# Layer 1's softmax sums: a pair's first eight blocks summed by VectorE in place of TensorE

## The chip, the cores and the metric

The kernel runs on one core of a Trainium2 chip. The metric is the time of one execution on the device in microseconds (us). Before the change it was 3967.98 us (median of 3 runs, 3965.11 to 3968.51).

## The reference

Two graph layers run on 4096 nodes of 512 features; only the second matters here. It is a masked attention with 8 heads of 64:

```python
q = jnp.einsum('nd,hdk->hnk', node_matrix, Wqs)      # k, v alike
scores = jnp.einsum('hqk,hmk->hqm', q, k) * kd ** (-0.5)
scores = scores + IDENTITY_BIAS * eye - MASK_VAL * (1.0 - adj)
att = jax.nn.softmax(scores, axis=-1)
return jnp.einsum('hqm,hmk,hko->qo', att, v, Wo)
# then x = layernorm(x + that)
```

The softmax needs, for every query and head, the sum of the weights over all 4096 keys. The change is about who forms that sum.

## The kernel before

Queries are taken in 8 groups of 512, heads in 4 pairs. Such a "pair" `(g, m)` meets its keys in 32 blocks `j` of 128. For a block TensorE makes scores (keys on the partitions, queries along the free axis), ScalarE takes the exponential in place, VectorE multiplies by the mask into a weight tile `p` of 128 x 1024, and TensorE multiplies `p` by the values. A sum over keys is one over the 128 partitions and the 32 blocks. GpSimd adds 24 of the blocks elementwise into `q_sum`; TensorE sums the other eight straight from `p`, with a column of ones:

```python
def by_tensor(j):
    return j % 6 in (2, 3) and j < BY_PE              # BY_PE = 24: blocks 2 3 8 9 14 15 20 21

def weigh(g, m, j, s):
    nc.scalar.activation(s, s, AF.Exp)
    p = wp.tile([P, HP, G], F32, name="p1", bufs=10)
    # ... cut: the mask
    nc.vector.tensor_tensor(p, s, mask.to_broadcast([P, HP, G]), op=ALU.mult)
    pt[g, m, j] = p
    if by_tensor(j) or j == 0:
        return
    # ... cut: j == 1 starts q_sum
    nc.gpsimd.tensor_tensor(q_sum[g, m], q_sum[g, m], p, op=ALU.add)

def close1(g, t, s):                                  # finishes one output tile
    # ... cut: y = x + s on VectorE; mean and variance; 1/sd and nb on GpSimd
    nc.gpsimd.tensor_scalar(nb, nb, -1.0, None, op0=ALU.mult)

    def normalise():
        nc.scalar.activation(y, y, AF.Identity, bias=nb, scale=rs)
        nc.sync.dma_start(out[i * P:(i + 1) * P, :], y)
    later.at(2, normalise)
```

A step takes three blocks (the eleventh, the tail, takes two) and issues them in this order:

```python
got = [scores(*u) for u in batch]                     # three score buffers in all
# ... cut, in the tail: sums of the pair before, projection of one output tile
for u, su in zip(batch, got):
    weigh(*u, su)
if extra_sum:  divide(*extra_sum, den_ps)             # GpSimd: on = o_sb * r
if extra_tile: close1(*extra_tile, y_ps[:, 0, :])
for g, m, j in last:                                  # the batch of the step before
    products(g, m, j)
# ... cut: column sums, copy of the finished output
later.step()                                          # at(2): at the end of the next step
```

So the normalisation of a tile that closes in a tail stands, in ScalarE's program, behind the exponentials of the next pair's blocks 0 to 2 and ahead of those of blocks 3 to 5.

Of the kernel before, what the change touches and what calls it, by code (L numbers as in the profile page):

```python
# [8 lines left out]
F32 = mybir.dt.float32  # L9
BF16 = mybir.dt.bfloat16  # L10
I32 = mybir.dt.int32
AF = mybir.ActivationFunctionType
ALU = mybir.AluOpType
AX = mybir.AxisListType
# [3 lines left out]
P = 128  # L18
# [411 lines left out]
def tile_gat_then_masked_attention(  # L430
# [16 lines left out]
    nc = tc.nc  # L447
    N, D = x.shape
    H0, D0, _ = weight_u.shape
    H1, _, KD = wks.shape  # L450
    NT = N // P
    G = 512
# [2 lines left out]
    KC = D // P  # L455
    HP = P // KD
    NP1 = H1 // HP
    QD = P // 4
    CH = 8
    NCH = NT // CH  # L460
    W0 = D0 + 1
# [9 lines left out]
    const = main.enter_context(tc.tile_pool(name="const", bufs=1))  # L471
# [9 lines left out]
    ones = const.tile([P, KD], F32, name="ones")  # L481
# [2 lines left out]
    nc.vector.tensor_scalar(ident_e, ident, 1.0100501670841679, None, op0=ALU.mult)  # L484
    least = const.tile([P, NG * NP1], F32, name="least")
    total = const.tile([P, NG * NP1], F32, name="total")
    pick = const.tile([P, HP, KD], F32, name="pick")
    nc.gpsimd.memset(pick, 0.0)
    for e in range(HP):
        for n in range(2):  # L490
            r = (n * HP + e) * QD
            nc.gpsimd.memset(pick[r:r + 1, e, :], 1.0)

    base_d = [dram.tile([P, D], F32, name=f"base_d{i}") for i in range(NT)]
    x1_d = [dram.tile([P, D], F32, name=f"x1_d{i}") for i in range(NT)]
# [31 lines left out]
    with tc.tile_pool(name="l0", bufs=1) as l0, \  # L527
# [41 lines left out]
        with tc.tile_pool(name="l0s", bufs=2) as sp, \  # L569
# [56 lines left out]
            for g in range(NG):  # L626
# [4 lines left out]
                for c in range(KC):  # L631
                    p = ps.tile([P, GT, P], F32, name="t_ps")
# [9 lines left out]
                for t in range(GT):  # L642
# [3 lines left out]
                    for c in range(KC):  # L646
                        nc.tensor.matmul(s_ps, xT[:, c, t * P:(t + 1) * P], w_sb[:, c, :],
                                         start=(c == 0), stop=(c == KC - 1))
                    b_ps = ps.tile([P, D], F32, name="b_ps")
                    for c in range(KC):  # L650
                        nc.tensor.matmul(b_ps, xT[:, c, t * P:(t + 1) * P], pw_sb[:, c, :],
                                         start=(c == 0), stop=(c == KC - 1))
# [6 lines left out]
                    for k, f in ((0, f1[:, i, :]), (1, f2[:, i, :])):  # L659
# [3 lines left out]
                                                op=ALU.mult)  # L663
# [19 lines left out]
        with tc.tile_pool(name="l0w", bufs=2) as wp, \  # L683
# [3 lines left out]
            fr_t, sup_t, agg_t, az_t, o_t, p_t = {}, {}, {}, {}, {}, {}  # L687
# [95 lines left out]
            for n, (w, h, j) in enumerate(steps):  # L783
# [6 lines left out]
                u = h * NT + j  # L790
# [3 lines left out]
                p = p_t.pop((w, h, j))  # L794
                for t in range(WT):
                    nc.tensor.matmul(o[t // BK][:, t % BK, :], p[:, t * P:(t + 1) * P],  # L796
                                     sup_t[w, h][:, j, :],
                                     start=(j == 0 and t % BK == 0), stop=(j == NT - 1),
# [9 lines left out]
    with tc.tile_pool(name="l1", bufs=1) as l1:  # L808
        wo_sb = l1.tile([P, KC, D], F32, name="wo_sb")

        with tc.tile_pool(name="l1s", bufs=2) as sp, \
# [17 lines left out]
            for g in range(NG):  # L829
# [4 lines left out]
                for m in range(NP1):  # L834
                    k_ps = ps.tile([P, G], F32, name="k_ps")
                    for c in range(KC):
                        nc.tensor.matmul(k_ps, w3["wk"][:, c, m * P:(m + 1) * P], xT[:, c, :],  # L837
                                         start=(c == 0), stop=(c == KC - 1))
# [4 lines left out]
                    for c in range(KC):  # L843
                        nc.tensor.matmul(q_ps, w3["wq"][:, c, m * P:(m + 1) * P], xT[:, c, :],  # L844
                                         start=(c == 0), stop=(c == KC - 1))
# [4 lines left out]
                for t in range(GT):  # L850
                    v_ps = ps.tile([P, D], F32, name="v_ps")
                    for c in range(KC):
                        nc.tensor.matmul(v_ps, xT[:, c, t * P:(t + 1) * P], w3["wv"][:, c, :],
                                         start=(c == 0), stop=(c == KC - 1))
# [8 lines left out]
        with tc.tile_pool(name="l1w", bufs=2) as wp, \  # L863
                tc.tile_pool(name="l1p", bufs=1, space=PSUM) as ps:
            NB = 3
            BY_PE = 24
            kt, vt, qt, at, mdt, pt, q_sum, o_t, o_sb, sm_t, sm_sb, on_t = (
                {} for _ in range(12))
            later = Later()

# [4 lines left out]
            def of_group(g, j0, j1):  # L875
                r = g * G % W
                return adjT_d[g * G // W][:, j0:j1, r:r + G]

            def load_adjT(g, c):
                at[g, c] = wp.tile([P, CH, G], BF16, name="adjT1", bufs=NCH + 2)  # L880
                nc.sync.dma_start(at[g, c], of_group(g, c * CH, (c + 1) * CH))

            def load_md(g):
# [53 lines left out]
                                     start=True, stop=True)  # L937
                return s

            def by_tensor(j):  # L940

                return j % 6 in (2, 3) and j < BY_PE

            def weigh(g, m, j, s):
                nc.scalar.activation(s, s, AF.Exp)  # L945
                p = wp.tile([P, HP, G], F32, name="p1", bufs=10)
                if j // GT == g:
                    mask = mdt[g][:, j % GT, None, :]
                else:
                    mask = at[g, j // CH][:, j % CH, None, :]  # L950
                nc.vector.tensor_tensor(p, s, mask.to_broadcast([P, HP, G]), op=ALU.mult)  # L951
                pt[g, m, j] = p
                if by_tensor(j) or j == 0:
                    return
                if j == 1:
                    q_sum[g, m] = wp.tile([P, HP, G], F32, name="q_sum")
                    nc.gpsimd.tensor_tensor(q_sum[g, m], pt[g, m, 0], p, op=ALU.add)
                else:
                    nc.gpsimd.tensor_tensor(q_sum[g, m], q_sum[g, m], p, op=ALU.add)  # L959

            def products(g, m, j):
                if j == 0:
                    o_t[g, m] = ps.tile([P, G], F32, name="o1_ps")
                o = o_t[g, m]
                p = pt[g, m, j]
                v = vt[g, m, j // CH]
                for e in range(HP):
                    r = slice(e * KD, (e + 1) * KD)
                    nc.tensor.matmul(o[r, :], v[:, j % CH, r], p[:, e, :],  # L969
                                     start=(j == 0), stop=(j == NT - 1))  # L970

            def sums(g, m, j):


                if j == 3:
                    sm_t[g, m] = ps.tile([P, G], F32, name="sm_ps")
                for n in range(2):
                    for e in range(HP):
                        r = (n * HP + e) * QD
                        nc.tensor.matmul(sm_t[g, m][r:r + QD, :], ones[:, 0:QD],  # L980
                                         pt[g, m, j - 1 + n][:, e, :],
                                         start=(j == 3), stop=(j + 6 >= BY_PE))

            def all_sums(g, m, s):
                q = q_sum.pop((g, m))
                sm = sm_sb.pop((g, m))
                for e in range(HP):
                    nc.tensor.matmul(s[e * KD:(e + 1) * KD, :], ones, q[:, e, :],
                                     start=True, stop=False)
                for e in range(HP):  # L990
                    nc.tensor.matmul(s[e * KD:(e + 1) * KD, :], pick[:, e, :], sm,
                                     start=False, stop=True)

            def divide(g, m, s):
                if m == 0:
                    on_t[g] = wp.tile([P, NP1, G], F32, name="on")
                den = wp.tile([P, G], F32, name="den1")
                nc.scalar.activation(den, s, AF.Copy)
                r = wp.tile([P, G], F32, name="r1")
                n = index[g, m, 0] // NT  # L1000

                nc.vector.tensor_reduce(least[:, n:n + 1], den, AX.X, ALU.min)  # L1002
                nc.vector.tensor_reduce(total[:, n:n + 1], den, AX.X, ALU.add)  # L1003
                nc.vector.reciprocal(r, den)  # L1004
                nc.gpsimd.tensor_tensor(on_t[g][:, m, :], o_sb.pop((g, m)), r, op=ALU.mult)  # L1005
# [5 lines left out]

            def close1(g, t, s):
                i = g * GT + t
                y = wp.tile([P, D], F32, name="y1", bufs=4)
                nc.sync.dma_start(y, x1_d[i])
                nc.vector.tensor_tensor(y, y, s, op=ALU.add)  # L1016

                mv, rs = moments(y)
                nb = small.tile([P, 1], F32, name="nb")
                nc.gpsimd.tensor_tensor(nb, mv[:, 0:1], rs, op=ALU.mult)  # L1020
# [6 lines that stand above are left out]
# [7 lines left out]
            def step(batch, extra_sum, extra_tile):  # L1034
                got = [scores(*u) for u in batch]
                if extra_sum:
                    den_ps = ps.tile([P, G], F32, name="sm_ps")
                    all_sums(*extra_sum, den_ps)
                if extra_tile:
                    y_ps = ps.tile([P, HP, G], F32, name="s_ps", bufs=NB)  # L1040
                    project(*extra_tile, y_ps[:, 0, :])
                for u, su in zip(batch, got):
                    weigh(*u, su)
                if extra_sum:
                    divide(*extra_sum, den_ps)
                if extra_tile:
                    close1(*extra_tile, y_ps[:, 0, :])
                for g, m, j in last:
                    products(g, m, j)
                for g, m, j in last:  # L1050
                    if by_tensor(j) and j % 6 == 3:
                        sums(g, m, j)
                        if j + 6 >= BY_PE:
                            sm_sb[g, m] = wp.tile([P, G], F32, name="sm_sb")
                            nc.scalar.activation(sm_sb[g, m], sm_t.pop((g, m)), AF.Copy)
                    if j == NT - 1:
                        o_sb[g, m] = wp.tile([P, G], F32, name="o_sb")
                        nc.scalar.activation(o_sb[g, m], o_t.pop((g, m)), AF.Copy)
                last[:] = batch
                later.step()  # L1060
# [66 lines left out]
```

## Time and profile before

| | before |
|---|---|
| median of the runs | 3968.12 us |
| TensorE busy (PE) | 3799.8 us, 96% |
| VectorE (DVE) / ScalarE (ACT) / GpSimd (POOL) busy | 2532.6 / 1855.8 / 2046.3 us |
| one pair of layer 1, with a tile to close | 68.29 us |

Busy shares are averages over two layers with different limits. The useful unit is one pair, read from the timeline of each engine; the lines are in the prediction. In such a line the first number is the start in us from the start of the span, the second the time to the end of a merged run, and what stands in brackets is the idle time ahead of the run and what ended it.

### The profile page before, as it was taken

The numbers are of one execution on the slowest core, as the hardware profiler recorded it, in microseconds if no ns is written. First come the engines' busy times: TensorE is split into PE (matmuls) and PEld (weight loads), VectorE is DVE, ScalarE is ACT, GpSimd is POOL, SyncE is SP. The second block draws the span as 40 slices with busy tenths as digits, with TensorE's granted clock in tenths as the row PEclk, the third lists the DMA queues.
The fourth block names the chain that finished last, engine by engine and source line by source line (L and its number), as shares of the span: only waits on it lengthen the run. The fifth ranks groups of instructions, "written<-read, shape, count | busy, mean of one in ns | idle before, by whom it ended". The sixth has DMA issues, their size and how long they took to land. (4 is left out here: it accounts for less than half of the span.)

```text
span 3967.4 us, 51832 instructions
## 1 busy us (share of the span) xinstructions
PE 3799.8 (96%) x20490; PEld 1985.2 (50%) x20490; DVE 2532.6 (64%) x2432; ACT 1855.8 (47%) x2113; POOL 2046.3 (52%) x1211
## 2 busy tenths in 40 slices
PE   7988998999989889989999999999999999999998
PEld 3448998989989734433333333333333333333332
DVE  3447998988989801125666666666666666666665
ACT  1226767767656510024444444444444444444443
POOL 2320012021030100018888888888887888888886
PEclk9998999999999989999999999999999999999999
DMA  6885566656431143242222322322323223223211
GB/s 163 193 199 162 131 195 157 175 161 160 150 109 63 43 148 111 98 146 83 96 83 80 117 83 79 113 88 78 109 74 114 80 88 117 80 77 115 75 63 54
DMA packets 232429, 447.47 MB, mean 113 GB/s; under 512 B 21744, under 2 KB 136688, under 8 KB 225008
## 3 DMA queue, kind: packets, MB, share of 16 engines
q1 hardware_dynamic: 179264, 386.38, 29.4%
q0 software_dynamic: 42432, 51.39, 7.8%
q10 hardware_dynamic: 10480, 6.29, 0.5%
q8 instruction: 163, 2.67, 0.3%
q14 instruction: 90, 0.74, 0.1%
HBM read 372.51 MB, written 100.86 MB: 119 GB/s over the span
## 5 line engine op out<-in xcount | busy, mean ns | idle before, releaser
L959 POOL TENSOR_TENSOR q_sum<-q_sum,p 128x1024 f32<-128x1024 f32 x704 | 1659.0, 2356 | 332.6 <-DVE p L951 287.2
L951 DVE TENSOR_TENSOR p<-s_ps,adjT 128x1024 f32<-128x1024 f32 x896 | 1043.8, 1217 | 686.1 <-ACT s_ps L945 669.1
L945 ACT ACTIVATE s_ps<-s_ps 128x1024 f32<-128x1024 f32 x1024 | 971.1, 1009 | 1004.2 <-PE s_ps L936 1004.1
L796 PE MATMUL o_ps<-sup_t,p 128*128 128x129 f32 x8192 | 966.0, 279 | 42.4 <-DVE p L719 42.4
L936 PE MATMUL s_ps<-q_sb,k_sb 64*128 64x512 f32 x4096 | 981.6, 610 | 16.8 <-issue 10.2
L796 PEld LDWEIGHTS o_ps<-sup_t,p 128*128 128x128 f32 x8192 | 941.5, 194 | 52.2 <-issue 29.6
L969 PE MATMUL o_ps<-p,v_sb 128*64 128x512 f32 x4096 | 956.5, 601 | 0.0
L936 PEld LDWEIGHTS s_ps<-q_sb,k_sb 64*128 64x128 f32 x4096 | 367.6, 187 | 628.4 <-issue 388.4
L719 DVE SCALAR_TENSOR_TENSOR p<-fr_t,dj,az 128x1024 f32<-128x1024 f32 x512 | 635.5, 1280 | 27.7 <-DVE az L715 0.9
L712 ACT ACTIVATE z<-fr_t,f1s 128x1024 bf16<-128x1024 f32 x512 | 555.5, 1141 | 132.8 <-DVE az L715 106.3
L969 PEld LDWEIGHTS o_ps<-p,v_sb 128*64 128x64 f32 x4096 | 263.1, 136 | 649.7 <-issue 621.3
L715 DVE TENSOR_TENSOR az<-adjT,z 128x2048 bf16<-128x2048 bf16 x256 | 311.6, 1217 | 88.4 <-ACT z L712 88.2
L752 POOL DMA_DIRECT2D agg<-base_d x32 | 29.0, 1120 | 443.2 <-ACT agg L740 442.8
L538 POOL DMA_DIRECT2D arow<-in_adj_dram x32 | 30.7, 960 | 402.0 <-PE at_ps L553 402.0
L560 ACT ACTIVATE stage<-at_ps 128x1024 bf16<-128x1024 bf16 x128 | 130.7, 1021 | 206.5 <-PE at_ps L553 200.9
L951 DVE TENSOR_TENSOR p<-s_ps,md 128x1024 f32<-128x1024 f32 x128 | 150.4, 1216 | 94.7 <-ACT s_ps L945 93.4
L886 POOL DMA_DIRECT2D md<-adjT_d x8 | 6.6, 824 | 354.9 <-DMA v_d<-vg 354.6
L840 DVE COPY kg<-k_ps 128x512 f32<-128x512 f32 x32 | 22.1, 692 | 196.2 <-PE k_ps L837 190.1
L980 PE MATMUL sm_ps<-p,ones 128*32 128x512 f32 x1024 | 136.4, 605 | 0.0
L847 ACT ACTIVATE qg<-q_ps 128x512 f32<-128x512 f32 x32 | 19.1, 597 | 237.4 <-PE q_ps L844 237.4
L837 PE MATMUL k_ps<-xT,wk 128*128 128x512 f32 x256 | 118.1, 605 | 12.5 <-DMA xT<-x1T_d 12.5
L661 DVE TENSOR_TENSOR prod<-sup,uv 128x512 f32<-128x512 f32 x64 | 51.7, 807 | 117.6 <-ACT sup L657 117.6
(91 smaller groups left out, 2107.3 us busy)
## 6 DMA issues: line engine op xcount, KB each, us to landing
adjT<-adjT_d SPq DMA_DIRECT2D x64, 1024.0 KB, 7.1
k_sb<-k_d SPq DMA_DIRECT2D x128, 512.0 KB, 3.5
v_sb<-v_d SPq DMA_DIRECT2D x128, 512.0 KB, 3.6
sup_t<-sup_d SPq DMA_DIRECT2D x16, 2064.0 KB, 13.1
arow<-in_adj_dram POOLq DMA_DIRECT2D x32, 1024.0 KB, 12.5
adjT_d<-stage SPq DMA_DIRECT2D x64, 512.0 KB, 5.7
fr_t<-fr_d SPq DMA_DIRECT2D x16, 1024.0 KB, 8.9
sup_d<-sup SPq DMA_DIRECT2D x32, 258.0 KB, 10.9
```

Of the source, the lines that this page charges most:

```text
L560: nc.scalar.activation(s[:, j % 2, :], p.rearrange("p t r -> p (t r)"), AF.Copy)
L712: nc.scalar.activation(z[:, k, :], fr[:, 0, :], AF.Abs, bias=f1s[:, j + k, h:h + 1], scale=BIG)
L715: nc.vector.tensor_tensor(az, adjT[w, j // CJ][:, j % CJ:j % CJ + 2, :], z, op=ALU.min)
L719: nc.vector.scalar_tensor_tensor(p, fr[:, 1, :], dj[:, j, h:h + 1], az_t[w, h, j // 2][:, j % 2, :], op0=ALU.max, op1=ALU.mult)
L796: nc.tensor.matmul(o[t // BK][:, t % BK, :], p[:, t * P:(t + 1) * P], sup_t[w, h][:, j, :], start=(j == 0 and t % BK == 0), stop=(j == NT ...
L837: nc.tensor.matmul(k_ps, w3["wk"][:, c, m * P:(m + 1) * P], xT[:, c, :], start=(c == 0), stop=(c == KC - 1))
L936: nc.tensor.matmul(s[:, e, :], k[r, a:a + P], qt[g, m][r, :], start=True, stop=True)
L945: nc.scalar.activation(s, s, AF.Exp)
L951: nc.vector.tensor_tensor(p, s, mask.to_broadcast([P, HP, G]), op=ALU.mult)
L959: nc.gpsimd.tensor_tensor(q_sum[g, m], q_sum[g, m], p, op=ALU.add)
L969: nc.tensor.matmul(o[r, :], v[:, j % CH, r], p[:, e, :], start=(j == 0), stop=(j == NT - 1))
L980: nc.tensor.matmul(sm_t[g, m][r:r + QD, :], ones[:, 0:QD], pt[g, m, j - 1 + n][:, e, :], start=(j == 3), stop=(j + 6 >= BY_PE))
```

## The change

The intent: TensorE is the bound, VectorE is idle for a third of the time. So VectorE takes over TensorE's eight blocks. It writes their weights side by side in one buffer and later adds eight elements along the free axis with a `tensor_reduce`, an eighth of the queries per step. The eight blocks become the first eight of the pair, so that they are complete early, and GpSimd adds blocks 9 to 31 to block 8.

```diff
-            BY_PE = 24
+            NV = 8
 ...
-                p = wp.tile([P, HP, G], F32, name="p1", bufs=10)
+                if j < NV:
+                    if j == 0:
+                        p8_t[g, m] = wp.tile([P, NV, HP, G], F32, name="p8", bufs=1)
+                    p = p8_t[g, m][:, j]
+                else:
+                    p = wp.tile([P, HP, G], F32, name="p1", bufs=8)
 ...
-                if by_tensor(j) or j == 0:
-                    return
-                if j == 1:
+                if j == NV + 1:
                     q_sum[g, m] = wp.tile([P, HP, G], F32, name="q_sum")
 ...
-                else:
+                elif j > NV:
                     nc.gpsimd.tensor_tensor(q_sum[g, m], q_sum[g, m], p, op=ALU.add)
+
+            def add_up(g, m, k):
+                if k == 0:
+                    v_sum[g, m] = wp.tile([P, HP, G], F32, name="v_sum")
+                w = HP * G // 8
+                c = slice(k * w, (k + 1) * w)
+                nc.vector.tensor_reduce(
+                    v_sum[g, m].rearrange("p e r -> p (e r)")[:, c],
+                    p8_t[g, m].rearrange("p u e r -> p (e r) u")[:, c, :], AX.X, ALU.add)
 ...
+                if batch and batch[0][2] > NV:
+                    add_up(batch[0][0], batch[0][1], (batch[0][2] - NV) // NB)
```

Cut: the functions that made the column sums, the closing matmuls (as many as before), and smaller numbers of some buffers (`adjT1` 6 to 5, `y1` 4 to 3, `den1` and `r1` 2 to 1), which make room for the 32 KB that `p8` takes in each partition.

More of the change, by code (lines that the diff above doesn't have):

```diff
@@ L457, in tile_gat_then_masked_attention @@
     NP1 = H1 // HP
-    QD = P // 4
     CH = 8
@@ L486, in tile_gat_then_masked_attention @@
     total = const.tile([P, NG * NP1], F32, name="total")
-    pick = const.tile([P, HP, KD], F32, name="pick")
-    nc.gpsimd.memset(pick, 0.0)
-    for e in range(HP):
-        for n in range(2):
-            r = (n * HP + e) * QD
-            nc.gpsimd.memset(pick[r:r + 1, e, :], 1.0)
     base_d = [dram.tile([P, D], F32, name=f"base_d{i}") for i in range(NT)]
@@ L865, in tile_gat_then_masked_attention @@
             NB = 3
-            BY_PE = 24
-            kt, vt, qt, at, mdt, pt, q_sum, o_t, o_sb, sm_t, sm_sb, on_t = (
+            NV = 8
+            kt, vt, qt, at, mdt, pt, p8_t, q_sum, v_sum, o_t, o_sb, on_t = (
                 {} for _ in range(12))
@@ L879, in load_adjT @@
             def load_adjT(g, c):
-                at[g, c] = wp.tile([P, CH, G], BF16, name="adjT1", bufs=NCH + 2)
+                at[g, c] = wp.tile([P, CH, G], BF16, name="adjT1", bufs=NCH + 1)
                 nc.sync.dma_start(at[g, c], of_group(g, c * CH, (c + 1) * CH))
@@ L938, in scores @@
                 return s
-            def by_tensor(j):
-                return j % 6 in (2, 3) and j < BY_PE
             def weigh(g, m, j, s):
                 nc.scalar.activation(s, s, AF.Exp)
-                p = wp.tile([P, HP, G], F32, name="p1", bufs=10)
+                if j < NV:
[4 more added lines that the diff above has]
+                    p = wp.tile([P, HP, G], F32, name="p1", bufs=8)
                 if j // GT == g:
@@ L952, in weigh @@
                 pt[g, m, j] = p
-                if by_tensor(j) or j == 0:
-                    return
-                if j == 1:
+                if j == NV + 1:
                     q_sum[g, m] = wp.tile([P, HP, G], F32, name="q_sum")
-                    nc.gpsimd.tensor_tensor(q_sum[g, m], pt[g, m, 0], p, op=ALU.add)
-                else:
+                    nc.gpsimd.tensor_tensor(q_sum[g, m], pt[g, m, NV], p, op=ALU.add)
+                elif j > NV:
                     nc.gpsimd.tensor_tensor(q_sum[g, m], q_sum[g, m], p, op=ALU.add)
+            def add_up(g, m, k):
[6 more added lines that the diff above has]
+                    p8_t[g, m].rearrange("p u e r -> p (e r) u")[:, c, :], AX.X, ALU.add)
             def products(g, m, j):
@@ L970, in products @@
                                      start=(j == 0), stop=(j == NT - 1))
-            def sums(g, m, j):
-                if j == 3:
-                    sm_t[g, m] = ps.tile([P, G], F32, name="sm_ps")
-                for n in range(2):
-                    for e in range(HP):
-                        r = (n * HP + e) * QD
-                        nc.tensor.matmul(sm_t[g, m][r:r + QD, :], ones[:, 0:QD],
-                                         pt[g, m, j - 1 + n][:, e, :],
-                                         start=(j == 3), stop=(j + 6 >= BY_PE))
             def all_sums(g, m, s):
                 q = q_sum.pop((g, m))
-                sm = sm_sb.pop((g, m))
-                for e in range(HP):
-                    nc.tensor.matmul(s[e * KD:(e + 1) * KD, :], ones, q[:, e, :],
-                                     start=True, stop=False)
-                for e in range(HP):
-                    nc.tensor.matmul(s[e * KD:(e + 1) * KD, :], pick[:, e, :], sm,
-                                     start=False, stop=True)
+                v = v_sum.pop((g, m))
+                for n, part in enumerate((q, v)):
+                    for e in range(HP):
+                        nc.tensor.matmul(s[e * KD:(e + 1) * KD, :], ones, part[:, e, :],
+                                         start=(n == 0), stop=(n == 1))
             def divide(g, m, s):
@@ L996, in divide @@
                     on_t[g] = wp.tile([P, NP1, G], F32, name="on")
-                den = wp.tile([P, G], F32, name="den1")
+                den = wp.tile([P, G], F32, name="den1", bufs=1)
                 nc.scalar.activation(den, s, AF.Copy)
-                r = wp.tile([P, G], F32, name="r1")
+                r = wp.tile([P, G], F32, name="r1", bufs=1)
                 n = index[g, m, 0] // NT
@@ L1013, in close1 @@
                 i = g * GT + t
-                y = wp.tile([P, D], F32, name="y1", bufs=4)
+                y = wp.tile([P, D], F32, name="y1", bufs=3)
                 nc.sync.dma_start(y, x1_d[i])
@@ L1050, in step @@
                 for g, m, j in last:
-                    if by_tensor(j) and j % 6 == 3:
-                        sums(g, m, j)
-                        if j + 6 >= BY_PE:
-                            sm_sb[g, m] = wp.tile([P, G], F32, name="sm_sb")
-                            nc.scalar.activation(sm_sb[g, m], sm_t.pop((g, m)), AF.Copy)
                     if j == NT - 1:
```

## The prediction

The 264 and 684 ns are VectorE `tensor_reduce`s of neighbouring elements in the trace of before (128 x 128, lines 680 and 681, and 128 x 512, line 1002). That GpSimd's adds would keep their 2.36 us beside the reductions was the assumption; no run had shown it. The rival's 2.3 us for a strided reduction is a supposition too, close to what twice the measured slope gives: 684 - 512 x 1.09 = 126 ns, and 126 + 1024 x 2.18 = 2358 ns. The 0.07 and 0.1 us for a signal are allowances.

> **What bounds the kernel now.** I read the page first, then the costliest groups, then the timeline of one pair of layer 1, engine by engine. The page says who is busy:
>
> ```profile
> PE 3799.8 (96%) x20490; PEld 1985.2 (50%) x20490; DVE 2532.6 (64%) x2432; ACT 1855.8 (47%) x2113; POOL 2046.3 (52%) x1211
> ...
> L959 POOL TENSOR_TENSOR q_sum<-q_sum,p 128x1024 f32<-128x1024 f32 x704 | 1659.0, 2356 | 332.6 <-DVE p L951 287.2
> L951 DVE TENSOR_TENSOR p<-s_ps,adjT 128x1024 f32<-128x1024 f32 x896 | 1043.8, 1217 | 686.1 <-ACT s_ps L945 669.1
> ...
> L980 PE MATMUL sm_ps<-p,ones 128*32 128x512 f32 x1024 | 136.4, 605 | 0.0
> ```
>
> PE (TensorE) is the bound. The last group is what the change removes. The first is GpSimd's 736 block sums (704 here, and 32 that open a pair), 23 in each of 32 pairs.
>
> A pair is 32 blocks: ten steps of three and a tail of two. The timeline of TensorE gives the period of a step (start of scores to start of scores):
>
> ```profile
> 2845.19 2.85 PE L936 MATMUL s_ps<-q_sb,k_sb 64*128 64x512 f32 x12
> 2847.97 2.80 PE L969 MATMUL o_ps<-p,v_sb 128*64 128x512 f32 x12
> 2850.69 1.07 PE L980 MATMUL sm_ps<-p,ones 128*32 128x512 f32 x8
> 2851.69 2.85 PE L936 MATMUL s_ps<-q_sb,k_sb 64*128 64x512 f32 x12
> ```
>
> 2845.19 to 2851.69 is 6.50 us with column sums; a step without them takes 5.50 (2839.69 to 2845.19). The sums cost 1.00 us, four times a pair. The same timeline has 4.64 for a pair's first step (2835.05 to 2839.69) and 10.15 for the tail (2824.90 to 2835.05). A pair is 4.64 + 9 x 5.50 + 4 x 1.00 + 10.15 = 68.29 us, without a gap on PE.
>
> The timelines of GpSimd and then ScalarE around the same end of a pair (the next begins at 2835.05):
>
> ```profile
> 2800.12 9.67 POOL L959 TENSOR_TENSOR q_sum<-q_sum,p 128x1024 f32<-128x1024 f32 x4 [2.26 <-DVE p L951]
> 2812.12 24.29 POOL L959 TENSOR_TENSOR q_sum<-q_sum,p 128x1024 f32<-128x1024 f32 x10 [2.33 <-DVE p L951]
> 2836.36 1.27 POOL L1005 TENSOR_TENSOR on<-o_sb,r 128x512 f32<-128x512 f32 x1
> ...
> 2838.93 0.23 POOL L1021 TENSOR_SCALAR nb<-nb 128x1 f32<-128x1 f32 x1
> ```
>
> ```profile
> 2839.87 0.60 ACT L1058 ACTIVATE o_sb<-o_ps 128x512 f32<-128x512 f32 x1 [0.80 <-PE o_ps L969]
> 2840.36 0.81 ACT L1024 ACTIVATE y<-y,nb,bn_rs 128x512 f32<-128x512 f32 x1
> 2841.06 2.84 ACT L945 ACTIVATE s_ps<-s_ps 128x1024 f32<-128x1024 f32 x3
> ```
>
> These decide the prediction. GpSimd adds four blocks and rests, four times; only the last ten are back to back, and they end 1.3 us into the next pair. Behind them in its queue stand the product `on` and the statistics of an output tile, ending with `nb` at 2839.16. ScalarE's normalisation of that tile needs `nb`, and stands in ScalarE's queue ahead of the next pair's exponentials of blocks 3 to 5. It comes up at 2840.36: 1.2 us of slack.
>
> [...] 264 ns for 128 elements, 684 ns for 512, a slope of 1.09 ns. [...] the new reduction steps 4096 bytes between the elements that it adds, and I found no such VectorE read in this trace. [...] (the columns after PE, PEld, DVE, ACT and POOL busy are PEclk, DMA share, GB/s):
>
> ```profile
> 1744.00:1748.00 4.00, 0.00 (x0) 0.00 (x0) 0.00 (x0) 0.00 (x0) 0.45 (x1) 0.73 0.71 213
> 1748.00:1752.00 4.00, 0.14 (x2) 0.17 (x3) 0.00 (x0) 0.00 (x0) 0.31 (x1) 0.50 1.10 329
> 1752.00:1756.00 4.00, 4.00 (x10) 1.83 (x12) 0.00 (x0) 1.33 (x2) 0.00 (x0) 0.50 1.24 375
> ```
>
> A gap of 4.21 us at 3938.5 also led to a clock of 0.56. After such gaps twelve score matmuls took 4.94 and 4.43 us instead of 2.85, so half clock lasted about (4.94 - 2.85) x 2 = 4.2 and 3.2 us of running; I use 4.0.
>
> **The change part by part.**
> *Removed:* 32 column-sum matmuls a pair, 4 x 1.00 us on the path, 32 x 4.0 = 128 us in all; and a ScalarE copy of 0.60 us, off the path.
> *Added:* eight VectorE reductions a pair over 1024 inputs each: 684 + 512 x 1.09 = 1.24 us, an estimate from the two durations above. They fall behind the three products (3.49 us) of the steps 3 to 10: 4.73 us of a 5.50 us step, so they fit. The closing matmuls are as many as before.
> *Moved:* GpSimd still adds 23 times, but now blocks 9 to 31 in one run, where eight blocks that it skipped used to lie in between. A step brings three adds, 3 x 2.44 = 7.3 us against 5.50 of arrivals. Spacing: (24.29 - 2.36) / 9 = 2.44.
>
> Follow it from S, the start of the scores of blocks 9 to 11. In the trace a product begins 2.29 us after its step's scores and takes 1.22, and the add follows 0.13 later: the chain starts at S + 3.64. Ten adds took 24.24 us to the start of `on`, so 23 take 24.24 + 13 x 2.44 = 55.9: `on` starts at S + 59.6. From there to the end of `nb` the trace has 2.80 us: S + 62.4. The normalisation starts about 0.07 later, the exponential of block 3 0.70 after that, its product 1.11 later, done in 1.22; with 0.1 for the signal the score buffer of block 3 is free at S + 65.6.
>
> TensorE without any wait would get there earlier. From S to the next pair's start it needs 7 x 5.50 + 10.15 = 48.65, then 4.64 + 5.50 to the scores of blocks 6 to 8, which reuse that buffer (there are three): S + 58.8. So it stands 6.8 us. That is long enough for half clock: two of the 2.85 us of scores are done in 4.0 us, the rest in 0.85; the products take 2.72. The next S comes at 65.6 + 4.85 + 2.72 = 73.1 us, against 68.3 now: +4.8 us a pair. Without the clock, scores would follow the products' pace of 1.16 us, 3.3 us in all, and the period would be 71.6: +3.3.
>
> *The sum.* Output tiles close in the tails from the sixth pair on, so 26 starts of pairs pay the 4.84 (73.13 - 68.29, before rounding): +126. The first pairs, which have no such tile, gain: 1 us before the first S, 5 x 4.0 between, 3 in the last pair after its S: -24. At the end the last sums wait for GpSimd and the last denominators for one more normalisation, which I put 8 us later than now, by the same addition. 3968 + 126 - 24 + 8 = 4078 us.
>
> **The rivals.**
> *Off the path is gained in full:* 3968 - 128 = 3840 us. For it: PE has no gap now and VectorE has room. Against it: 1.2 us of slack before a queue that will come 9 us later. It needs GpSimd's lag not to reach ScalarE.
> *The strided reduction is slow and VectorE becomes the bound:* [...] a step costs 3.49 + 2.3 = 5.8 us, 0.3 over TensorE. Alone it would eat 2 to 3 of the 4 us: about 3920. But TensorE's 6.8 us of waiting absorb it, as the reductions lie outside the loop above; I give it no weight beside that loop.
> *Reductions hold GpSimd up:* if each blocked an add for its 1.24 us, the chain would be up to 8 x 1.24 = 10 us longer and the time near 4078 + 260 = 4340. [...]
> *The buffers of `p1`, eight instead of ten, stop VectorE:* block 31 takes the buffer of block 23, whose add ends at S + 3.64 + 15 x 2.44 = 40.2; the product is due at S + 38.5 + 3.45 = 42.0. 1.8 us to spare.
>
> **Range and chances.** Without the clock's fall: 4078 - 26 x 1.5 = 4039. With a half clock one and a half microseconds longer, and slightly slower adds: about 4115. If a link of the chain is misread, the result lies far below, near 3840. I say 4025 to 4115; slower by over 2% (above 4047) 0.72, within 2% 0.18, faster 0.10.
>
> **What would show it.** Right: in the profile after, ScalarE's `y` waits for POOL `nb` some 8 us, 26 times; PE's scores wait for DVE `p` near 7 us once a pair, with the clock low behind them; POOL shows runs of 23 adds of 55 to 56 us; the pairs early in layer 1 take 4 us less, the later ones about 73 us. Wrong: `y` starts without a wait, or the adds' mean is far from 2.36 us, or PE has no gap. A reduction of about 1.24 us would clear the stride, one near 2.3 convict it, with little effect on the time.

## The result, and the profile after

The changed kernel takes 4077.84 us (median of 4 runs, 4077.14 to 4081.3), 2.8% more. The ratio is 1.028 (95% interval 1.0262 to 1.0298). A ratio here is the mean time of one kernel's fast runs over that of the other's fast runs of the same rounds, so it is not quite the ratio of the two medians.

The page after, its line of engines and the groups that answer to those shown of before:

```profile
PE 3745.1 (92%) x19466; PEld 1983.1 (49%) x19466; DVE 3016.4 (74%) x2688; ACT 1845.0 (45%) x2081; POOL 2049.8 (50%) x1206
...
L951 POOL TENSOR_TENSOR q_sum<-q_sum,p 128x1024 f32<-128x1024 f32 x704 | 1663.5, 2363 | 55.2
...
L959 DVE TENSOR_REDUCE v_sum<-p 128x128 f32<-128x1024 f32 x256 | 494.9, 1933 | 0.0
...
L1012 ACT ACTIVATE y<-y,nb,bn_rs 128x512 f32<-128x512 f32 x32 | 26.0, 812 | 248.6 <-POOL nb L1009 248.6
```

The column sums are gone, and yet no engine has become the bound: TensorE is busy 92% of a longer span, VectorE 74%. GpSimd's additions cost what they did (2363 ns against 2356), but their idle time ahead fell from 332.6 to 55.2 us, as they now stand back to back. The reduction takes 1933 ns. The last line is the sign: ScalarE's normalisation of `y` now waits 248.6 us for GpSimd's `nb`.

The timeline of GpSimd and then of ScalarE over one end of a pair:

```profile
2892.12 2.36 POOL L949 TENSOR_TENSOR q_sum<-p,p 128x1024 f32<-128x1024 f32 x1 [14.05 <-DVE p L945]
2894.56 53.59 POOL L951 TENSOR_TENSOR q_sum<-q_sum,p 128x1024 f32<-128x1024 f32 x22
2948.11 1.26 POOL L993 TENSOR_TENSOR on<-o_sb,r 128x512 f32<-128x512 f32 x1
...
2950.68 0.23 POOL L1009 TENSOR_SCALAR nb<-nb 128x1 f32<-128x1 f32 x1
```

```profile
2941.94 0.60 ACT L1043 ACTIVATE o_sb<-o_ps 128x512 f32<-128x512 f32 x1 [0.74 <-PE o_ps L971]
2950.95 0.81 ACT L1012 ACTIVATE y<-y,nb,bn_rs 128x512 f32<-128x512 f32 x1 [8.41 <-POOL nb L1009]
2951.67 2.83 ACT L934 ACTIVATE s_ps<-s_ps 128x1024 f32<-128x1024 f32 x3
```

And TensorE's:

```profile
2944.60 2.79 PE L971 MATMUL o_ps<-p,v_sb 128*64 128x512 f32 x12
2953.98 5.49 PE L929 MATMUL s_ps<-q_sb,k_sb 64*128 64x512 f32 x12 [6.59 <-DVE p L945]
2959.40 3.11 PE L971 MATMUL o_ps<-p,v_sb 128*64 128x512 f32 x12
```

GpSimd ends its run of 23 at 2948.15 and `nb` at 2950.91. ScalarE has stood since 2942.5, starts `y` 0.04 us after `nb`, and only then takes the exponential of block 3. TensorE stood 6.59 us for a score buffer, although what it is said to wait for is VectorE's `p`: VectorE had nothing to multiply, as ScalarE stood (its product at 2952.70 starts after 9.82 us without work, which end with ScalarE's exponential). Behind the gap the twelve score matmuls take 5.49 us in place of 2.85. The windows view gives the clock there (columns as in the prediction):

```profile
2948.00:2952.00 4.00, 0.00 (x0) 0.00 (x0) 0.00 (x0) 1.05 (x2) 3.41 (x7) 0.73 0.00 0
2952.00:2956.00 4.00, 2.02 (x6) 0.94 (x8) 3.30 (x3) 2.49 (x3) 0.00 (x0) 0.50 1.10 312
2956.00:2960.00 4.00, 4.00 (x12) 1.16 (x10) 2.56 (x3) 2.50 (x3) 0.00 (x0) 0.50 0.95 363
```

From 2960 on it is 0.99, so TensorE ran at half clock for about 6 us after its restart at 2953.98. In the pair before it restarted at 2881.14, after an equal gap of 6.57 us, and ran at half clock for 3.9 us only:

```profile
2881.00:2885.00 4.00, 3.87 (x10) 1.76 (x12) 3.04 (x4) 1.69 (x3) 0.00 (x0) 0.50 0.64 247
2885.00:2889.00 4.00, 4.00 (x18) 1.11 (x18) 2.88 (x3) 1.93 (x2) 0.00 (x0) 1.00 0.47 135
```

The two kinds take turns, and with them periods of about 73.9 and 72.8 us. Six of the last 26 periods are shorter, about 71.7 us: there VectorE also finishes masks (see `late4_md`), and TensorE has a gap of 3.0 us in another place.

The copy of a pair's finished output (`o_sb`) happens once per pair, so the distances between its starts are the periods. The first starts at 1825.0 us before and at 1821.1 after; the last at 3934.1 and 4038.4. Summed:

| stretch | before | after | difference |
|---|---|---|---|
| to the first copy | 1825.0 | 1821.1 | -3.9 |
| next 5 periods | 331.3 | 318.6 | -12.7 |
| last 26 periods | 1777.8 | 1898.7 | +120.9 |
| from the last copy to the end of the span | 33.3 | 41.1 | +7.8 |
| span of the profiled run | 3967.4 | 4079.5 | +112.1 |

The first row is no gain of the change: over all ten profiles that stretch takes 1815.1 to 1825.0 us, whichever kernel.

### The profile page after: what moved, and what is told of

Same layout as the page of the kernel before. It is cut to its first block, busy times and chain, and to the rows that moved or that the text cites. A ratio compares the mean times of both kernels' runs of the same rounds, so it can differ in the third digit from the quotient of the medians.

```text
span 4079.5 us, 49923 instructions
## 1 busy us (share of the span) xinstructions
PE 3745.1 (92%) x19466; PEld 1983.1 (49%) x19466; DVE 3016.4 (74%) x2688; ACT 1845.0 (45%) x2081; POOL 2049.8 (50%) x1206
## 5 line engine op out<-in xcount | busy, mean ns | idle before, releaser
L951 POOL TENSOR_TENSOR q_sum<-q_sum,p 128x1024 f32<-128x1024 f32 x704 | 1663.5, 2363 | 55.2
L929 PE MATMUL s_ps<-q_sb,k_sb 64*128 64x512 f32 x4096 | 1044.8, 642 | 178.5 <-DVE p L945 168.3
L929 PEld LDWEIGHTS s_ps<-q_sb,k_sb 64*128 64x128 f32 x4096 | 384.3, 196 | 822.2 <-DVE p L945 522.5
L959 DVE TENSOR_REDUCE v_sum<-p 128x128 f32<-128x1024 f32 x256 | 494.9, 1933 | 0.0
L949 POOL TENSOR_TENSOR q_sum<-p,p 128x1024 f32<-128x1024 f32 x32 | 75.6, 2363 | 419.2 <-DVE p L945 419.2
L1012 ACT ACTIVATE y<-y,nb,bn_rs 128x512 f32<-128x512 f32 x32 | 26.0, 812 | 248.6 <-POOL nb L1009 248.6
```

The lines of the kernel that those rows point to most:

```text
L929: nc.tensor.matmul(s[:, e, :], k[r, a:a + P], qt[g, m][r, :], start=True, stop=True)
L949: nc.gpsimd.tensor_tensor(q_sum[g, m], pt[g, m, NV], p, op=ALU.add)
L959: nc.vector.tensor_reduce(v_sum[g, m].rearrange("p e r -> p (e r)")[:, c], p8_t[g, m].rearrange("p u e r -> p (e r) u")[:, c, :], AX.X, AL ...
```

## The experiments

The theory: moving GpSimd's work into one run makes `nb` late, `nb` stops ScalarE's queue, and that stops TensorE. The main rival: the strided reduction, 1.93 us and not 1.24, loads VectorE too much. All runs are of one kernel beside the kernel before on the same chip (medians of before: 3965.36 us in the first four, 3968.27 in the others). A first draft of `late4`, with three `y1` buffers, deadlocked in simulation (the reason was not shown); with a fourth buffer it ran, correct.

### `moved_alone`: the order of GpSimd's work without the reductions

```diff
 # on the kernel before
-                return j % 6 in (2, 3) and j < BY_PE      # BY_PE = 24
+                return j < BY_PE                          # BY_PE = 8
```

The start of `q_sum` goes to block 9, and the column sums follow blocks 1, 3, 5 and 7.

> The kernel before with one part of the change: TensorE still sums eight blocks with its column of ones, but now the first eight, so that GpSimd adds blocks 9 to 31 in one run; no VectorE reduction. Theory (the lag of GpSimd holds up ScalarE's queue): the loop of the prediction, 73.1 us, with two groups of column sums of 1.0 us each on its way (those behind the products of blocks 3 to 5), so about 75 us a pair; 26 times about 6.8 us more than before and 8 us at the end: some 4150 us; ScalarE's y waits for nb about 5 to 8 us, 26 times. Rival (VectorE's strided reductions cost the time): no reduction, no loss, 3968 us. The run before with the change gave 4078 us.

Measured: 4137.69 us (4136.53 to 4138.61), ratio 1.0432, correct. ScalarE's timeline and TensorE's in one pair:

```profile
2906.40 0.81 ACT L1024 ACTIVATE y<-y,nb,bn_rs 128x512 f32<-128x512 f32 x1 [7.23 <-POOL nb L1021]
```

```profile
2909.50 5.21 PE L936 MATMUL s_ps<-q_sb,k_sb 64*128 64x512 f32 x12 [4.54 <-DVE p L951]
2914.64 2.79 PE L969 MATMUL o_ps<-p,v_sb 128*64 128x512 f32 x12
2917.36 1.92 PE L980 MATMUL sm_ps<-p,ones 128*32 128x512 f32 x16
```

One part of the change, alone, makes the kernel 4.3% slower without a single VectorE reduction. The rival can't explain it. Of the 56 us that it is worse than the whole change (profiled runs), 12 lie in the first five periods, which keep their column sums (331.0 us; 331.3 in the kernel before), and 43 in the last 26, or 1.65 us each. There the column sums, 1.92 us, now lie behind the gap and so inside the loop; that this is the cause of the 1.65 us fits the lines, but was not tested alone.

### `late4`: ScalarE's normalisation two steps further on

```diff
 # on the kernel with the change
-                y = wp.tile([P, D], F32, name="y1", bufs=3)
+                y = wp.tile([P, D], F32, name="y1", bufs=4)
 ...
-                later.at(2, normalise)
+                later.at(4, normalise)
```

> The kernel with the change, in which only the normalisation of an output tile is issued two steps later in ScalarE's program (four steps after the tile is closed in place of two; one buffer more for it). GpSimd's work and VectorE's reductions are as they were. Theory: nb is done 13.5 us after the start of a pair and ScalarE comes to the normalisation at about 14 us, so it waits no more than 1 us and TensorE's gap of 6.6 us goes: the 128 us of the column sums are gained, less 1 us in 5 pairs and about 3 us in the 8 pairs in which VectorE also finishes a mask: 3860 to 3885 us. Rival (the reductions of 1.93 us make VectorE the bound, or eight buffers for the products are too few): still above 3950 us.

Measured: 3877.22 us (3872.25 to 3879.06), ratio 0.9777, correct. GpSimd is as late as before, but nobody stands in line behind it:

```profile
2860.09 2.84 ACT L934 ACTIVATE s_ps<-s_ps 128x1024 f32<-128x1024 f32 x3 [2.66 <-PE s_ps L929]
2862.82 0.82 ACT L1012 ACTIVATE y<-y,nb,bn_rs 128x512 f32<-128x512 f32 x1
```

Most pairs now take 64.30 us; 68.29 - 4 x 1.00 is 64.29. So one number in the program, with a buffer to allow it, takes back the loss, and the gain that was sought appears. This also fixes what the reductions cost: with GpSimd's queue out of the way their 1.93 us fit into the steps, by a hair. The same kernel's VectorE timeline:

```profile
2872.20 3.49 DVE L945 TENSOR_TENSOR p<-s_ps,adjT 128x1024 f32<-128x1024 f32 x3 [0.17 <-ACT s_ps L934]
2875.61 1.93 DVE L959 TENSOR_REDUCE v_sum<-p 128x128 f32<-128x1024 f32 x1
2877.71 1.22 DVE L945 TENSOR_TENSOR p<-s_ps,adjT 128x1024 f32<-128x1024 f32 x1 [0.17 <-POOL q_sum L951]
```

From 2872.20 to 2877.71 is one step, 5.51 us, and VectorE idles 0.17 us of it.

### `before_late4`: the same edit on the kernel before

```diff
 # on the kernel before
-                later.at(2, normalise)
+                later.at(4, normalise)
```

> The kernel before, with nothing but the normalisation issued two steps later: the control for the run with four steps. Theory: before the change y did not wait for nb (1.2 us of slack), so nothing is gained: 3966 us, within 8 us. Rival (the later normalisation is itself a gain, and the 3877 us owe nothing to the change): up to 100 us less.

Measured: 3966.3 us, ratio 0.9997 (0.9981 to 1.0014), correct. The later normalisation is worth nothing by itself; it pays only where `nb` is late.

### `late3`: the middle dose

The same edit on the kernel with the change, with `later.at(3, normalise)` and three buffers.

> The kernel with the change, the normalisation issued one step later (three after the closing in place of two). It is the middle dose between the change (4078 us) and four steps (3877 us). Theory: ScalarE comes to the normalisation 8.7 us after the pair's start, nb is done at 13.75, so y waits about 5 us; the exponential of block 6, due at 11.3, starts at about 14.5, and its buffer is free some 2 us less late than that because a step has 2 us of room: TensorE's gap is 1.5 to 2.5 us in place of 6.6, and the time is 3877 + 26 x 2 = about 3930 us (3910 to 3960). Rival (a queue position matters only once, or not): equal to one of the two.

Measured: 3901.31 us (3900.76 to 3902.22), ratio 0.9833, correct: between the two, and below the range that I gave. The mechanism was as expected and the size was not:

```profile
2876.80 0.81 ACT L1012 ACTIVATE y<-y,nb,bn_rs 128x512 f32<-128x512 f32 x1 [4.57 <-POOL nb L1009]
2877.52 2.82 ACT L934 ACTIVATE s_ps<-s_ps 128x1024 f32<-128x1024 f32 x3
```

```profile
2879.83 3.39 PE L929 MATMUL s_ps<-q_sb,k_sb 64*128 64x512 f32 x12 [0.55 <-DVE p L945]
```

The exponential started 13.95 us after the pair's start (2863.57), not 14.5, so TensorE's gap was 0.55 us, with another 0.54 from scores that follow VectorE's pace (3.39 against 2.85). Ordinary periods are 65.4 to 66.0 us in place of 64.3. A wait of 4.57 us on ScalarE cost 1.1 us on TensorE, one of 8.41 about 9 (73.4 us a pair against 64.3): only what exceeds the room in the step counts, and then the clock comes on top.

### `skip3`: three additions fewer (wrong result)

```diff
-                elif j > NV:
+                elif j > NV and j not in (12, 18, 24):
```

> The kernel with the change, in which GpSimd leaves out three of its 23 additions (blocks 12, 18 and 24), so that the denominators are wrong on purpose. VectorE's and TensorE's work are unchanged. Theory: the run of additions is 3 x 2.44 = 7.3 us shorter, the wait of y for nb falls from 8.4 us to about 1, TensorE's gap of 6.6 us goes: 3860 to 3890 us. Rival (VectorE's reductions, or GpSimd's own busy time with no queue behind it): a change in GpSimd's work moves nothing, about 4078 us.

Measured: 3863.59 us, ratio 0.9743; the result is wrong (relative error 0.43). The wait of `y` is now 1.0 to 1.3 us in each of the 26 pairs in place of 8.4, and most periods are 64.30 us, as in `late4`:

```profile
2853.14 0.81 ACT L1012 ACTIVATE y<-y,nb,bn_rs 128x512 f32<-128x512 f32 x1 [1.13 <-POOL nb L1009]
```

GpSimd is busy for 50% of the span with the change, and for about 47% here (an estimate: 2049.8 us less 96 additions of 2.36 us, of 3860.7), so here it was not its busy time that counted but when its run ended.

### `contig`: the reductions without the stride (wrong result)

```diff
-                    p8_t[g, m].rearrange("p u e r -> p (e r) u")[:, c, :], AX.X, ALU.add)
+                    p8_t[g, m].rearrange("p u e r -> p (u e r)")[:, k * NV * w:(k + 1) * NV * w]
+                    .rearrange("p (a u) -> p a u", u=NV), AX.X, ALU.add)
```

> The kernel with the change, in which each reduction reads 1024 neighbouring elements in place of 1024 that lie 4096 bytes apart (128 sums of 8 as before, but of the wrong elements: a wrong result on purpose). It measures what the stride costs: if the stride is the reason for 1.93 us, the reduction falls to the 1.24 us that I had worked out from contiguous ones; if it is the eight-element groups or the 128 outputs, it stays near 1.9. Theory: VectorE's time lies outside the loop, so the kernel stays at 4078 us, within 10, in either case. Rival (VectorE's reductions cost the time): 8 x 0.7 us x 32 pairs = 180 us less, about 3900 us.

Measured: 4069.16 us (4067.33 to 4072.82), ratio 1.026, wrong result (relative error 0.65). The group of the reductions:

```profile
L959 DVE TENSOR_REDUCE v_sum<-p 128x128 f32<-128x1024 f32 x256 | 309.4, 1209 | 0.0
```

The stride is the reason for 1933 ns: the same 128 sums of eight take 1209 ns from neighbouring elements. That is 0.7 ns more for each of the 1024 elements, 1.6 times as long; only this one stride was tried. That frees 494.9 - 309.4 = 185.5 us of VectorE, and the kernel becomes 9 us faster. In the pairs that pay the loss, VectorE's time lies outside the loop: the last 26 periods are 5.5 us shorter in all, 0.2 us each, while VectorE has 5.8 us less to do in each. In the early pairs without a tile to close it shows; TensorE's scores at the start of such a pair, with the change and then here:

```profile
1950.38 3.39 PE L929 MATMUL s_ps<-q_sb,k_sb 64*128 64x512 f32 x12 [1.03 <-DVE p L945]
1945.46 3.39 PE L929 MATMUL s_ps<-q_sb,k_sb 64*128 64x512 f32 x12 [0.27 <-DVE p L945]
```

The gap falls from 1.03 to 0.27 us and the period from 62.16 to 61.41.

### `filler`: useless matmuls in TensorE's gap

```diff
 # on the kernel with the change, behind products()
+                if last and last[0][2] == 0 and index[last[0]] // NT >= NP1 + 2:
+                    fill = ps.tile([P, G], F32, name="sm_ps")
+                    for _ in range(6):
+                        nc.tensor.matmul(fill, wo_sb[:, 0, 0:P], wo_sb[:, 1, :],
+                                         start=True, stop=True)
```

> The kernel with the change, with six useless full matmuls (12 instructions of 0.46 us, 5.5 us in all) put into TensorE's gap of 6.6 us, behind the products of blocks 0 to 2, in the pairs that have the gap. They don't touch the wait for the exponentials; they only keep TensorE working. Theory (1.5 us of the loss per pair is the half clock behind the gap): twelve score matmuls behind the gap take about 3.3 us in place of 4.7 to 5.5, the mean granted clock goes from 0.96 to about 0.98, the time falls by 26 x 1.0 to 1.5 us to about 4045 us (4035 to 4052). Rival (the clock costs nothing, or the useless work itself delays): 4078 us or above.

Measured: 4053.59 us (4052.43 to 4067.95), ratio 1.0228, correct, just above the range that I gave. The mean granted clock went from 0.959 to 0.983. ScalarE's wait is unchanged (8.36 us in the pair below), but:

```profile
2935.47 5.42 PE L1043 MATMUL sm_ps<-wo_sb 128*128 128x512 f32 x12
2942.07 3.39 PE L929 MATMUL s_ps<-q_sb,k_sb 64*128 64x512 f32 x12 [1.18 <-DVE p L945]
```

The scores behind the gap take 3.39 us in place of 4.7 to 5.5, and ordinary pairs take 71.45 us; after the change they took 73.4 (mean of the 19 periods that no mask disturbs, 72.8 to 73.9). So doing 5.4 us of useless work saves 1.95 us a pair, the price of the clock. The total fell by only 24 us, as in the pairs in which masks are finished TensorE's gap is in another place, and there the matmuls are in the way: those periods rose from about 71.7 to between 73.3 and 74.7.

### `late4_md`: the masks at a moment when GpSimd rests

In `late4` one pair in four still took 67.95 to 69.34 us. There VectorE finishes the diagonal masks of the next group, four operations with two SBUF inputs each. The tile view of them (durations as least, median and greatest):

```profile
L885 DVE TENSOR_TENSOR md<-md,ident_e x32: 277/283/2430, 1752.5 to 3443.7; 128x128 f32<-128x128 f32 x32
```

The trace of the kernel with the change, which has the same groups of four, shows them one by one. In the group at 2137.11 the first takes 1.59 us and the third 2.43, and each ends 0.15 us after an addition of GpSimd does (at 2138.55 and 2141.11); the other two take 0.28. In the group at 1757.11, where GpSimd is not at work, all four take 0.28 to 0.29. So the long ones go with GpSimd's additions; what holds them is not shown.

```diff
 # on late4
-                if m == 2 and j == 0 and g + 1 < NG:
+                if m == 2 and j == 9 and g + 1 < NG:
                     finish_md(g + 1)
```

> The kernel with the change and the normalisation four steps on, in which VectorE also finishes the diagonal masks of the next group at block 9 of a pair in place of block 0. In the run with four steps one pair in four took 68 to 69 us in place of 64.3, and there the four small mask operations, each with two inputs in SBUF, took 4.4 us in a moment when GpSimd was adding, one of them 2.4 us long where the others take 0.28. At block 9 GpSimd stands idle and VectorE has 2 us to spare. Theory: all those pairs take 64.3 us: 7 x 4.5 = 31 us less, 3845 us (3838 to 3855). Rival (the masks' time is their own): no change, 3877 us.

Measured: 3845.99 us (3844.49 to 3847.32), ratio 0.9692 (0.9675 to 0.9708), correct: the fastest kernel of this study, 3.1% faster than before. The same view:

```profile
L885 DVE TENSOR_TENSOR md<-md,ident_e x32: 278/282/292, 1756.6 to 3431.0; 128x128 f32<-128x128 f32 x32
```

The longest of the 32 is now 292 ns, and 24 of the last 26 periods are 64.30 us. In `late4` the four took 4.35 us together (at 2915.28); now each takes 0.28 (median). Block 9 is also a place where VectorE has time to spare (2.08 us of idle time ahead of the products at 2866.70 in `late4`); how much of the gain is owed to that and how much to the end of the long operations is not separated.

## Why the prediction was right

The prediction gave 4078 us in 4025 to 4115; it came to 4077.84. Its first sign is there too: `y` waits 8.4 to 8.7 us for `nb` in 26 pairs. The steps, in the prediction's order, against the pair shown above, whose S is 2888.53:

| step | predicted | measured |
|---|---|---|
| chain of additions starts | S + 3.64 | S + 3.59 |
| `on` starts | S + 59.6 | S + 59.58 |
| `nb` ends | S + 62.4 | S + 62.38 |
| scores of block 6 start | S + 65.6 | S + 65.45 |
| TensorE's gap | 6.8 us | 6.59 us |
| next S | S + 73.1 | S + 73.91 (half clock lasted into the products; about 72.8 in the pairs of the other kind) |
| 26 late periods together | +126 | +120.9 |
| early part | -24, of which 3 in the last pair | -12.7 in the five periods, for which -20 was predicted; the -3.9 before them is within the scatter; the last pair counted among the 26 |
| the end | +8 | +7.8 |

**Bound, removed.** TensorE was the bound and the column sums cost 4.0 us a pair. `late4` shows it: 64.30 us against 68.29, when nothing else is in the way.

**Added: the term that was mis-sized.** "684 + 512 x 1.09 = 1.24 us" measured 1933 ns; `contig` shows that 0.72 us of it is the stride, which the prediction could not size, and that 1.24 was right without it. The second rival of the prediction had put it at 2.3. Why it did not move the result is shown by `contig` too. It did shrink the early gain: pairs without a tile to close fell from 64.50 to 62.16 us and not to 60.5, with a gap of 1.03 us on TensorE in each. That the longer last reduction in the tail makes the reciprocal and the next pair's products late agrees with this, and so does `contig`: reductions that are 0.72 us shorter take about 0.75 us off both the gap and the period. No run shortened that last reduction alone.

**Moved.** This was the decisive step, and it is shown three ways: done alone it costs 4.3%; with the queue behind it rearranged the loss is gone; with three additions fewer it is gone too.

**Clock.** The prediction gave 1.5 us a pair to the half clock, from 4.0 us of running at it (read behind gaps of 10.17 and 2.92 us, not only of the kind that it foresaw); `filler` shows 1.95 in ordinary pairs. By the clock records of the trace TensorE ran at half clock for 3.8 to 3.9 us in every other ordinary pair, as predicted, and for 6.0 to 6.2 us in the rest. That the sum met its mark to a microsecond is luck: ordinary pairs lost 5.1 us and not 4.84, the six with masks, which the prediction did not tell apart, 3.2, and the early part gained less.

**Rivals.** Full gain at 3840 us fell because the lag did reach ScalarE; with the queue mended, the kernel comes to 3846. GpSimd was not held up: 2363 ns against 2356. The eight `p1` buffers did not bind: VectorE's waits for `q_sum` are 9.8 us in all, none over 0.2.

## What to carry to other kernels

Here work that was taken off the bound was a gain only where what moved with it still ended in time: 4077.84 us with `nb` late in ScalarE's queue, 3877.22 with the queue rearranged, from 3968 before. Ask of each engine not how busy it is but when its last instruction of a round ends, and who stands in whose queue behind it. A small instruction that needed a late result held up what stood behind it in its engine's queue: an 0.81 us normalisation came after 8.41 us of waiting, and the exponential behind it started only then (2950.95 and 2951.67). Issuing it two steps later cost one buffer. When a gap on TensorE is several microseconds long, look for half clock behind it; here it cost 1.95 us a pair (`filler`). By the clock records of the traces of before and after, from 1740 us on, half clock began in each of the 37 gaps of 2.92 us or more, or within 1.7 us of its end, and with none of the three of about 1.8 us or with shorter ones. That is a count and not a threshold: in `late4`, by count of its clock records, it came behind four of six gaps of about 3.05 us.
